# A corner table stored as two shifted halves, and later samples' moments through one buffer, in a four-layer image network

## The chip, the cores and the metric

The kernel runs on one core of a Trainium2 chip. The metric is the device time of one execution in microseconds; the input is four samples of 96 channels by 128 x 128 pixels in float32, all computed by that core in one launch.

The engines named below: PE (matrix multiplication and transposition; PEld is its weight load), DVE (vector), ACT (activations), POOL (here gathers and some elementwise work), and SP, which issues nearly all DMAs. Each engine runs its instructions in the order in which they were put into its queue.

## The reference, cut to what matters

Four residual layers, each on a group-normalised input. Layer 2 is a deformable 3 x 3 convolution, and the change lies in what feeds it.

```python
x = x + _L0_conv_ref(_gn(x), ...)   # convolution, gate, two scans over all pixels
x = x + _L1_conv_ref(_gn(x), ...)   # spatial and spectral branches, 3x3 convolution
x = x + _L2_conv_ref(_gn(x), ...)   # deformable 3x3 convolution
x = x + _L3_conv_ref(_gn(x), ...)   # mask, DCT, state-space scans, DCT back

def _L2_conv_ref(x, weight, bias, offset_w, offset_b, mask_w, mask_b):
    offset = _conv(x, offset_w, offset_b)
    mask = jax.nn.sigmoid(_conv(x, mask_w, mask_b))
    ...
    for k in range(K * K):
        i, j = (k // K, k % K)
        dy = offset[:, 2 * k]
        dx = offset[:, 2 * k + 1]
        py = base_y[None, :, None] + i * DIL + dy
        px = base_x[None, None, :] + j * DIL + dx
        samp = _bilinear(x, py, px) * mask[:, k][:, None]
        out = out + jnp.einsum('bchw,oc->bohw', samp, weight[:, :, i, j])
    return out + bias[None, :, None, None]
```

`_bilinear` weighs four neighbouring pixels: (y, x), (y, x+1), (y+1, x), (y+1, x+1), zero outside the image.

## The kernel before, in words

Per sample there is a front (layers 0 and 1 and the offsets of layer 2: `front`, line 652), a back (the gather of layer 2, the mask and the first DCT of layer 3: `back`, line 1410) and `layer3` (the scans). The main loop at the end of `tile_net_kernel` runs: the first front alone; then, for each sample b, its back together with the front of sample b+1 (and the last DCT of sample b-1), followed by its layer 3 alone. The last back has no front beside it.

Front and back are written as generators, and every operation is recorded by `Program.record`; a planner (`Program.issue`) then puts the operations of the two lanes into one order per engine, by its own costs and by each operation's planned place within its lane. The order is fixed when the program is built; on the chip each engine follows it. All recorded operations carry line 66 in the profile (DMAs line 426), so they are told apart by the tiles' names.

The steps that the change touches:

- `layer0`, lines 662 to 755. `moments` (679) loads an image in eight pieces of 96 x 2048 (tile `l0_xt`) and takes `bn_stats` of each 512 columns, four per piece. It runs first for sample 0, in its own pool of three buffers. Then, in the first front only, `next_moments` (743) does the same for samples 1 to 3 in the pool `l0a`, three buffers too, beside the convolution of layer 0 (`block`, 719), which loads its rows, and stores its two results `u_d` and `sz_d`, through the same SP queue.
- `offsets`, lines 1247 to 1408. It goes over eight blocks of 16 rows. Each block loads 18 rows (`rows`, two buffers), normalises them on DVE, and builds the corner table `quad_d` in DRAM: one entry of 4 x 96 channels (1536 B) for each of 127 x 128 pixels, in the order (y, x), (y, x+1), (y+1, x), (y+1, x+1). Through `q4` (1254) it is written with the pixel's column x on the partitions.
- For every pair of rows PE transposes each row twice, once from column 0 and once from column 1, into one PSUM tile `l2_pt` (two buffers). DVE copies both halves of a row into the first two quarters of the tile `l2_qt` (three buffers, 128 x 4 rows x 384), and ACT copies the same into the last two quarters of the row before. Each four rows are stored by one DMA, 32 a sample.
- Between these, PE computes the offset convolution (`l2_po`), transposes it (`l2_pu`), and DVE and ACT make from it the row of the table to read (`idx_d`) and the four weights of each tap (`w4_d`), in the order of the corners (lines 1396 to 1405).
- `gather`, lines 1421 to 1524. POOL reads, for each image row and tap, one table entry per pixel by an indirect DMA into `l2_g`; `weigh` (1448) multiplies the four corners by their weights on ACT and adds on DVE; the result is transposed and multiplied by the layer's weights. The indices, weights and residual of the next four rows are fetched on the SP queue (`l2_i`, `l2_v`, `l2_x`).

The store of four rows before, with its only view of the table:

```python
q4 = T.quad_d.rearrange("(y x) e -> x y e", x=W)
...
nc.sync.dma_start(
    out=q4[:, BR * i + r - 4 : BR * i + r, :], in_=last
)
```

Of the kernel before, what the change touches and what calls it, by code (L numbers as in the profile page):

```python
# [23 lines left out]
F32 = mybir.dt.float32  # L24
# [3 lines left out]
ALU = mybir.AluOpType  # L28
# [4 lines left out]
C, H, W = 96, 128, 128  # L33
# [61 lines left out]
def staggered(jobs, gap):  # L95


    jobs = iter(jobs)
    active, wait = [], 0
    while True:  # L100
        if wait <= 0:
            job = next(jobs, None)
            if job is not None:
                active.append(job)
                wait = gap
        wait -= 1
        if not active:
            return
        for job in list(active):
            if next(job, "end") == "end":  # L110
                active.remove(job)
                if not active:
                    wait = 0
            else:
                yield
# [405 lines left out]
BR = 16  # L521
# [4 lines left out]
class Net:  # L526
# [135 lines left out]
    def layer0(self, xin, T, beside, ahead):  # L662
        nc, a = self.nc, self.a
# [3 lines left out]
        with self.program.pool(name="l0w", bufs=1) as wp, self.program.pool(name="l0p", bufs=1, space=PSUM) as ps:  # L667
# [8 lines left out]
            wc = wp.tile([C, 9, C], F32, name="l0_wc")  # L676
            nc.sync.dma_start(out=wc, in_=a["l0_cwT"].unsqueeze(0).to_broadcast([C, 9, C]))

            def moments(pool, x, st):
                for i in range(8):  # L680
                    xt = pool.tile([C, 2048], F32, name="l0_xt", tag="xt")
                    nc.sync.dma_start(out=xt, in_=x[:, i * 2048 : (i + 1) * 2048])
                    yield
                    for t in range(4):
                        nc.vector.bn_stats(st[:, 4 * i + t, :], xt[:, t * CH : (t + 1) * CH])
                        yield

            if ahead is not None:
                with self.program.pool(name="l0s", bufs=3) as wa:
                    yield from moments(wa, xin, st0)  # L690
# [26 lines left out]
            with self.program.pool(name="l0a", bufs=3) as wa, self.program.pool("l3i", 2) as wt:  # L717

                def block(i):
                    xb, cols = self.rows(wa, xin, i, 3)  # L720
                    yield
                    yield
                    nc.vector.tensor_scalar(xb[:, cols], xb[:, cols], scale, shift, ALU.mult, ALU.add)
                    yield
                    for r in range(3):
                        pc = ps.tile([128, CH], F32, name="l0_pc", tag="a", bufs=2)
                        yield from self.conv9(pc, wc, xb, i, r)
                        u = wa.tile([128, CH], F32, name="l0_u", tag="u")
                        nc.scalar.activation(u, pc, AF.Silu, bias=cb[:, r : r + 1], scale=1.0)
                        self.spread_out(u_d, u, i, r)  # L730
                        pz = ps.tile([128, CH], F32, name="l0_pz", tag="b", bufs=1)
                        with self.program.abreast():
                            for p, g, c in self.shares(r):
                                nc.tensor.matmul(
                                    out=pz[p : p + 32], lhsT=winT[:, C + c : C + c + 32],
                                    rhs=xb[:, W + g * CH : W + (g + 1) * CH], start=True, stop=True,
                                )
                        yield
                        sz = wa.tile([128, CH], F32, name="l0_sz", tag="sz")
                        nc.scalar.activation(sz, pz, AF.Silu)  # L740
                        self.spread_out(sz_d, sz, i, r)

                def next_moments():
                    for x, mv in ahead:
                        st = wa.tile([C, NCH, 6], F32, name="l0_st", tag="st", bufs=2)
                        yield from moments(wa, x, st)
                        nc.vector.bn_aggr(mv, st.rearrange("c n s -> c (n s)"))
                        yield

                jobs = [staggered((block(i) for i in range(NB)), 12)]  # L750
                if beside:
                    jobs.append(beside(ps, wt))
                if ahead:
                    jobs.append(next_moments())
                yield from staggered(jobs, 1)
# [491 lines left out]
    def offsets(self, T):  # L1247


        nc, a = self.nc, self.a  # L1250
# [3 lines left out]
        q4 = T.quad_d.rearrange("(y x) e -> x y e", x=W)  # L1254
        NR = BR + 3
        with self.program.pool(name="l2w", bufs=1) as wp, self.program.pool(name="l2a", bufs=2) as wa, self.program.pool(
            name="l2p", bufs=1, space=PSUM
# [15 lines left out]
            def block(i):  # L1273
                xb, cols = self.rows(wa, T.x2, i, pad=PAD)
# [5 lines left out]

                n = min(BR, H - 1 - BR * i)
                qt = None
                for r in range(0, n + 1, 2):
                    if r % 4 == 0 and r < n:
                        last, qt = qt, wa.tile([128, 4, 4 * C], F32, name="l2_qt", tag="qt", bufs=3)
                    elif r % 4 == 0:
                        last = qt
                    else:
                        last = qt
                    k = min(2, n + 1 - r)  # L1290
                    pt = ps.tile([128, 2, 2 * C], F32, name="l2_pt", tag="b", bufs=2)
                    for j in range(k):
                        for x in range(2):
                            c0 = (1 + r + j) * W + x
                            nc.tensor.transpose(
                                pt[:, j, x * C : (x + 1) * C], xb[:, c0 : c0 + W], self.ident[:C, :C]
                            )
                    yield
                    up = min(k, n - r)
                    if up > 0:  # L1300
                        nc.vector.tensor_copy(qt[:, r % 4 : r % 4 + up, 0 : 2 * C], pt[:, :up])
                    if r % 4:
                        nc.scalar.copy(qt[:, 1 : 1 + k, 2 * C : 4 * C], pt[:, :k])
                    else:
                        if r:
                            nc.scalar.copy(last[:, 3, 2 * C : 4 * C], pt[:, 0])
                            nc.sync.dma_start(
                                out=q4[:, BR * i + r - 4 : BR * i + r, :], in_=last
                            )
                        if k > 1:  # L1310
                            nc.scalar.copy(qt[:, 0, 2 * C : 4 * C], pt[:, 1])
                if n % 4:
                    nc.sync.dma_start(
                        out=q4[:, BR * i + n - n % 4 : BR * i + n, :], in_=qt[:, : n % 4]
                    )

                ot = wa.tile([128, NR, 123], F32, name="l2_ot", tag="ot")
                if prev[0] is None:
# [7 lines left out]
                for g in range(4):  # L1326
                    po = ps.tile([123, 4, W], F32, name="l2_po", tag="a", bufs=2)
                    x3 = image(xb[:, :XB])
                    for m, x in enumerate((0, -1, 1)):
                        ca, cb = max(0, -x), min(W, W - x)  # L1330
                        nc.tensor.matmul(
                            out=po[:, :, ca:cb], lhsT=woff[:, x + 1].rearrange("c y k -> c (y k)"),
# [7 lines left out]
                    pt = ps.tile([128, 4, 123], F32, name="l2_pu", tag="b", bufs=2)  # L1340
# [5 lines left out]
                r0 = 1 if i == 0 else 0  # L1346
                nr = BR + (i == NB - 1) - r0
                K9 = nr * 9
# [10 lines left out]
                w4 = wa.tile([128, NR * 9, 4], F32, name="l2_w4", tag="w4")  # L1359
                first, wts = [], []  # L1360
# [35 lines left out]
                for m in range(2):  # L1396
                    wy = wts[0][m]
                    wy3 = wy.rearrange("w (r k) -> w r k", k=9)
                    nc.vector.tensor_tensor(wy3, wy3, mask[:, :nr], ALU.mult)
                    for j in range(2):  # L1400
                        nc.vector.tensor_tensor(w4[:, :K9, 2 * m + j], wy, wts[1][j], ALU.mult)
                nc.sync.dma_start(
                    out=T.w4_d[:, row0 * 36 : row0 * 36 + 4 * K9],
                    in_=w4[:, :K9].rearrange("p k q -> p (k q)"),
                )
                yield

            yield from staggered((block(i) for i in range(NB)), 28)

    def back(self, T, alone=False):  # L1410
# [1040 lines left out]
```

## Time and profile before

| What | Value |
|---|---|
| Time, median of three runs | 14923.91 us (14919.98 to 14983.37) |
| The profiled execution's own time | 14956.1 us |
| Its span | 14954.0 us |
| Mean granted clock of PE | 0.894 |
| PE / DVE / ACT / POOL busy | 82% / 76% / 59% / 69% |
| Packets of the hardware queue (SP) | 1,013,872, 1972.56 MB, 45.8% of 16 DMA engines |
| Packets of the software queue (POOL's gathers) | 298,368, 906.38 MB, 20.5% |
| Stores of the corner table | 32 a sample; 768 KB for four rows |
| Offsets stage of sample 0 | first store issued at 1123.8, last at 1297.0 us; gather from 1318.0 us |
| Stores of samples 1, 2, 3 | 2916.0 to 3273.2, 6455.9 to 6850.0, 9974.9 to 10333.4 us |
| Gathers of samples 1, 2, 3 start | 4817.0, 8344.9, 11826.4 us |
| `bn_stats` of `l0_xt` for samples 1 to 3 | 51.8 to 153.9 us |

How to read the profile: "busy" is the time in which an engine worked on an instruction; waiting is not in it. In a group of instructions the columns are engine, operation, output <- inputs, shapes and count, then the busy time in us and the mean of one in ns, then the idle time of the engine just before these instructions and what ended it. Tile names stand without their digits: `l_qt` is `l2_qt`, `l_xt` is `l0_xt`; `l_pt<-ident,rows` are the transpositions for the corner table and `l_pt<-ident,l_sm` those of the gather. Names of the same letters in two layers fall together. A DMA's time on SP is that of its issue alone.

### The profile page before, as it was taken

Reading aid. Unit: us, or ns where it says so; the run is one execution under the profiler, and the core shown is the slowest. Engines: PE = TensorE matmul, PEld = TensorE weight load, DVE = VectorE, ACT = ScalarE, POOL = GpSimd, SP = SyncE. Lnnn points to the kernel's source line nnn. Section 1 sums busy time; section 2 is a strip of 40 time slices with the busy share of each in tenths; the row PEclk is TensorE's granted clock in tenths of the full one; section 3 lists DMA queues with packets and bytes.
Section 4 is the critical chain, followed back from the end, with each engine's and each line's share of the span. In section 5 each row is a group of like instructions: output and inputs, shape, how many; then the busy total and the mean of one; then the engine's idle time right before and its main releaser. Section 6 shows DMA issues by size and latency. Waiting matters only on the chain. (4 is left out here: it accounts for less than half of the span.)

```text
span 14954.0 us, 175601 instructions
## 1 busy us (share of the span) xinstructions
PE 12275.2 (82%) x48112; PEld 5769.1 (39%) x48112; DVE 11311.0 (76%) x21823; ACT 8881.9 (59%) x21508; POOL 10357.0 (69%) x7904
## 2 busy tenths in 40 slices
PE   7897787879998978878999878887999744459998
PEld 3353344343333434443333334534333422233334
DVE  4625686678998587677999678667999765558997
ACT  3614675556665586555666467555666465546664
POOL 2103747748998755765999774774999877758997
PEclk9998898979999988978999989888999855569999
DMA  6445658766666758875666766876666755556676
GB/s 163 135 131 187 185 168 249 233 205 177 188 196 192 243 169 225 236 221 162 194 189 193 222 202 176 255 237 186 192 189 196 213 171 168 166 153 184 187 199 193
DMA packets 1313229, 2890.16 MB, mean 193 GB/s; under 512 B 281008, under 2 KB 767600, under 8 KB 1197936
## 3 DMA queue, kind: packets, MB, share of 16 engines
q1 hardware_dynamic: 1013872, 1972.56, 45.8%
q0 software_dynamic: 298368, 906.38, 20.5%
q8 instruction: 381, 6.24, 0.2%
q14 instruction: 608, 4.98, 0.1%
HBM read 2455.55 MB, written 422.58 MB: 192 GB/s over the span
## 5 line engine op out<-in xcount | busy, mean ns | idle before, releaser
L66 POOL DMA_INDIRECT l_g<-quad_d,l_i x4608 | 4664.4, 1012 | 2516.9 <-issue 1330.6
L66 POOL TENSOR_TENSOR l_hc<-l_h,l_cl 128x1024 f32<-128x1024 f32 x1536 | 3608.5, 2361 | 288.6 <-DVE l_h L66 264.1
L66 PE MATMUL l_py<-l_hc,ident 128*128 128x512 f32 x6144 | 3073.9, 611 | 181.2 <-POOL l_hc L66 177.9
L66 DVE TENSOR_TENSOR_SCAN l_h<-l_dA,l_carry,l_dB 128x512 f32<-128x512 f32 x2304 | 2861.4, 1265 | 1.7
L66 ACT ACTIVATE l_dA<-l_dl,l_al 128x512 f32<-128x512 f32 x2304 | 1637.4, 718 | 1111.6 <-DVE l_h L66 1102.6
L66 DVE SCALAR_TENSOR_TENSOR l_sm<-l_g,l_v,l_sm 128x96 f32<-128x96 f32 x4608 | 1480.5, 322 | 1039.4 <-ACT l_sm L66 1004.6
L66 ACT ACTIVATE l_sm<-l_g,l_v 128x96 f32<-128x96 f32 x4608 | 1680.1, 369 | 646.8 <-DMA l_g<-quad_d,l_i 612.3
L66 ACT ACTIVATE l_part<-l_g,l_v 128x96 f32<-128x96 f32 x4608 | 1656.6, 364 | 213.3 <-DVE l_sm L66 213.1
L66 PEld LDWEIGHTS l_py<-l_hc,ident 128*128 128x128 f32 x6144 | 1135.2, 192 | 1348.3 <-issue 828.0
L66 PE MATMUL l_pc<-l_sT,l_wk 128*96 128x256 f32 (+1 forms) x3584 | 1238.3, 470 | 449.9 <-ACT l_sT L66 447.4
L66 DVE TENSOR_TENSOR l_dB<-l_du,l_pB 128x512 f32<-128x512 f32 x2304 | 1492.2, 677 | 48.7 <-POOL l_du L66 27.7
L66 PE MATMUL l_pB<-l_bc,pick 128*128 128x512 f32 x2304 | 1402.1, 637 | 136.1 <-DVE l_dB L66 122.1
L66 DVE SCALAR_TENSOR_TENSOR l_part<-l_g,l_v,l_part 128x96 f32<-128x96 f32 x4608 | 1477.8, 321 | 43.8 <-ACT l_part L66 43.1
L66 PE MATMUL l_pt<-ident,l_sm 128*128 128x128 f32 (+1 forms) x3584 | 793.7, 326 | 750.7 <-DVE l_sm L66 746.2
L66 POOL TENSOR_TENSOR l_dP<-l_du,l_cl 128x512 f32<-128x512 f32 x768 | 978.1, 1274 | 100.9 <-DMA l_cl<-bc_d 71.6
L66 DVE TENSOR_TENSOR_SCAN l_h<-l_dQ,l_carry,l_dP 128x512 f32<-128x512 f32 x768 | 971.1, 1264 | 58.1 <-POOL l_dP L66 54.7
L66 PEld LDWEIGHTS l_pc<-l_sT,l_wk 128*96 128x96 f32 (+1 forms) x3584 | 643.2, 199 | 962.4 <-ACT l_sT L66 552.2
L66 PEld LDWEIGHTS l_pt<-ident,l_sm 128*128 128x128 f32 (+1 forms) x3584 | 521.7, 164 | 1140.1 <-DVE l_sm L66 874.7
L66 ACT COPY l_sT<-l_pt 128x512 f32<-128x512 f32 (+1 forms) x1024 | 522.3, 522 | 626.8 <-PE l_pt L66 625.5
L66 POOL TENSOR_TENSOR l_du<-l_du,l_dl 96x512 f32<-96x512 f32 x256 | 339.9, 1328 | 792.8 <-DVE l_dl L66 482.5
L66 PE MATMUL l_pc<-rows,l_wc 96*32 96x508 f32 (+3 forms) x6912 | 841.7, 612 | 46.7 <-DVE rows L66 46.7
L66 PEld LDWEIGHTS l_pB<-l_bc,pick 128*128 128x128 f32 x2304 | 438.5, 191 | 1062.2 <-DVE l_dB L66 834.5
(274 smaller groups left out, 19887.2 us busy)
## 6 DMA issues: line engine op xcount, KB each, us to landing
l_cl<-bc_d SPq DMA_DIRECT2D x512, 1280.0 KB
l_cl<-bc_d SPq DMA_DIRECT2D x512, 640.0 KB
quad_d<-l_qt SPq DMA_DIRECT2D x124, 768.0 KB
l_g<-quad_d,l_i POOLq DMA_INDIRECT x4608
x<-l_x SPq DMA_DIRECT2D x352, 192.0 KB
l_uc<-u_d SPq DMA_DIRECT2D x256, 192.0 KB
l_x<-x SPq DMA_DIRECT2D x224, 192.0 KB
l_xs<-x SPq DMA_DIRECT2D x116, 256.0 KB
```

The lines of the kernel that those rows point to most:

```text
L66: ins = op(*args, **kw).ins
```

## The change

There are three edits.

1. `moments` takes the number of buffers, and `next_moments` calls it with one instead of three.
2. In `offsets` each row is transposed once, four rows into one PSUM tile (128 x 4 x 96, as many bytes as before). The tile `l2_qt` holds four rows of 192 channels, (y, x) and (y+1, x), half its former size, still in three buffers. DVE copies the rows, ACT the rows one further down. The table's entry has the order (y, x), (y+1, x), (y, x+1), (y+1, x+1). Each four rows are stored by the new function `put` with three DMAs on the SP queue: the tile from partition 0 into the first half of the entries, the tile from partition 1 (127 partitions) into the second half of the entries of columns 0 to 126, and the last partition into the second half of column 127, whose entries no index names, since the index is held to columns 0 to 126.
3. The weights are written in the new order of corners.

```diff
-            def moments(pool, x, st):
+            def moments(pool, x, st, bufs=3):
                 for i in range(8):
-                    xt = pool.tile([C, 2048], F32, name="l0_xt", tag="xt")
+                    xt = pool.tile([C, 2048], F32, name="l0_xt", tag="xt", bufs=bufs)
                     nc.sync.dma_start(out=xt, in_=x[:, i * 2048 : (i + 1) * 2048])
...
-                        yield from moments(wa, x, st)
+                        yield from moments(wa, x, st, 1)
...
-                for r in range(0, n + 1, 2):
-                    if r % 4 == 0 and r < n:
-                        last, qt = qt, wa.tile([128, 4, 4 * C], F32, name="l2_qt", tag="qt", bufs=3)
-                    elif r % 4 == 0:
-                        last = qt
-                    else:
-                        last = qt
-                    k = min(2, n + 1 - r)
-                    pt = ps.tile([128, 2, 2 * C], F32, name="l2_pt", tag="b", bufs=2)
+
+                def put(tile, r0, k):
+                    rows = slice(BR * i + r0, BR * i + r0 + k)
+                    nc.sync.dma_start(out=q4[:, rows, 0 : 2 * C], in_=tile[:, :k])
+                    nc.sync.dma_start(out=q4[0 : W - 1, rows, 2 * C : 4 * C], in_=tile[1:W, :k])
+                    nc.sync.dma_start(out=q4[W - 1 : W, rows, 2 * C : 4 * C], in_=tile[W - 1 : W, :k])
+
+                for r in range(0, n + 1, 4):
+                    k, up = min(4, n + 1 - r), min(4, n - r)
+                    last = qt
+                    pt = ps.tile([128, 4, C], F32, name="l2_pt", tag="b", bufs=2)
                     for j in range(k):
-                        for x in range(2):
-                            c0 = (1 + r + j) * W + x
-                            nc.tensor.transpose(
-                                pt[:, j, x * C : (x + 1) * C], xb[:, c0 : c0 + W], self.ident[:C, :C]
-                            )
-                    yield
-                    up = min(k, n - r)
+                        c0 = (1 + r + j) * W
+                        nc.tensor.transpose(pt[:, j, :], xb[:, c0 : c0 + W], self.ident[:C, :C])
+                    yield
                     if up > 0:
-                        nc.vector.tensor_copy(qt[:, r % 4 : r % 4 + up, 0 : 2 * C], pt[:, :up])
-                    if r % 4:
-                        nc.scalar.copy(qt[:, 1 : 1 + k, 2 * C : 4 * C], pt[:, :k])
-                    else:
-                        if r:
-                            nc.scalar.copy(last[:, 3, 2 * C : 4 * C], pt[:, 0])
-                            nc.sync.dma_start(
-                                out=q4[:, BR * i + r - 4 : BR * i + r, :], in_=last
-                            )
-                        if k > 1:
-                            nc.scalar.copy(qt[:, 0, 2 * C : 4 * C], pt[:, 1])
+                        qt = wa.tile([128, 4, 2 * C], F32, name="l2_qt", tag="qt", bufs=3)
+                        nc.vector.tensor_copy(qt[:, :up, 0:C], pt[:, :up])
+                    if r:
+                        nc.scalar.copy(last[:, 3, C : 2 * C], pt[:, 0])
+                        put(last, r - 4, 4)
+                    if k > 1:
+                        nc.scalar.copy(qt[:, : k - 1, C : 2 * C], pt[:, 1:k])
                 if n % 4:
-                    nc.sync.dma_start(
-                        out=q4[:, BR * i + n - n % 4 : BR * i + n, :], in_=qt[:, : n % 4]
-                    )
+                    put(qt, n - n % 4, n % 4)
...
-                        nc.vector.tensor_tensor(w4[:, :K9, 2 * m + j], wy, wts[1][j], ALU.mult)
+                        nc.vector.tensor_tensor(w4[:, :K9, 2 * j + m], wy, wts[1][j], ALU.mult)
```

## The prediction

> **What bounds the kernel now.** I first cut the span into stages (busy time of each engine by stretch: after the span, PE, PEld, DVE, ACT and POOL with counts, then granted clock, DMA share, GB/s).
>
> ```profile
> span 14954.0 us, 175601 instructions
> ...
> 1100.00:1320.00 220.00, 166.47 (x641) 95.77 (x633) 140.37 (x371) 81.56 (x207) 1.70 (x2) 0.75 0.51 168
> 1320.00:2880.00 1560.00, 1303.15 (x6882) 592.15 (x6882) 1062.29 (x2793) 968.97 (x2788) 1041.23 (x993) 0.91 0.71 206
> 2880.00:3300.00 420.00, 302.42 (x1122) 162.02 (x1122) 312.26 (x967) 257.17 (x778) 228.53 (x224) 0.76 0.69 217
> ...
> 3400.00:4800.00 1400.00, 1297.00 (x3188) 529.74 (x3188) 1340.39 (x1486) 924.36 (x1732) 1287.54 (x704) 0.98 0.66 190
> ```
>
> No engine bounds the whole. The reader is to see the first row: sample 0's offsets stage, alone on the core, no engine full, DMA at half its share. For samples 1 to 3 the same stage is mixed into the end of the previous sample's gather (2880 to 3300 and two like it); there POOL's gathers set much of the pace. The layer-3 scans (3400 to 4800) contain nothing that the change touches. So I read the offsets stage: the tile that changes, its PE work in the first front, and the DMA queue.
>
> ```profile
> L66 ACT COPY l_qt<-l_pt x380: 294/318/498, 1119.3 to 10332.2; 128x192 f32<-128x192 f32 x121, 128x384 f32<-128x384 f32 x69
> L66 DVE COPY l_qt<-l_pt x256: 339/550/579, 1118.7 to 10331.8; 128x384 f32<-128x384 f32 x128
> L426 SPq DMA_DIRECT2D quad_d<-l_qt x128: 359/370/1164, 1123.8 to 10333.4; - x128
> ...
>   DMA quad_d<-l_qt: 1.7, 2
> ```
>
> ```profile
> L66 PE MATMUL l_pt<-ident,rows 96*128 96x96 f32 x270 | 41.5, 298 | 24.6 <-ACT l_qt L66 17.6 <-DVE rows L66 6.9
> ```
>
> ```profile
> SPq L426 <- DVE l_idx L66: 75.9, 7, 11.2
> SPq L426 <- ACT l_qt L66: 54.4, 32, 3.8
> ```
>
> ```profile
> 1123.79 14.21 SPq L426 DMA_DIRECT2D quad_d<-l_qt  x4
> 1143.91 0.32 SPq L426 DMA_DIRECT2D rows<-x  x1
> 1153.81 0.34 SPq L426 DMA_DIRECT2D idx_d<-l_idx  x1
> 1156.04 0.33 SPq L426 DMA_DIRECT2D w_d<-l_w  x1
> 1156.94 5.20 SPq L426 DMA_DIRECT2D quad_d<-l_qt  x3
> ```
>
> What matters is the 1.7 us: in the whole run the three buffers of `qt` made engines wait 1.7 us for a store. The stores are free today; SP waits for the copies (54.4 us), not the copies for SP. A store's 512 packets of 1536 B are shared evenly: the trace's completion marks show sixteen reports for the store issued at 1123.79, 3.35 to 3.55 us later, and its packets take 65 ns (median; mean 69). 32 packets on each engine are 2.1 us; the other 1.3 us is latency.
>
> **The change, part by part.**
>
> *Transpositions and copies (saved).* 270 transpositions become 135: of 41.5 us PE in the first front 20.8 go, and perhaps half of the 24.6 us that they wait. DVE has 32 copies where it had 64 (0.55 us each: -17.6 us a sample). On ACT 192 columns take 0.32 us and 384 take 0.48, so 96 plus 288 take some 0.64 per four rows, 20 us a sample for 33 now. All three engines have room in this stage (166, 140 and 82 of 220 us), so this is worth at most the transpositions, 33 us in the first front, and less where the gather runs.
>
> *The stores (added).* Each `put` issues three DMAs for one. SP: 64 more per sample at 0.37 us, 24 us of a queue that spends far more waiting: nothing. The first (128 partitions) and the third (one partition, four rows) are harmless. The second, `tile[1:W]` into `q4[0 : W - 1]`, has 127 partitions, and the trace shows what an odd number of partitions does. Counting engine reports of one load each: 128 or 96 partitions report sixteen times; 65 (`k_fd`) thirteen; 12 (`rest`) twelve; 8 (`l1_m2`) eight; 6 partitions of 2 pieces (`l0_xpd`) six; 41 (`l2_boff`) **once**. The count is the largest divisor of the outer dimension up to 16. That the one engine works serially shows too: the 41 descriptors reported 1.76 us after issue, a single one (`l1_b2`) after 1.22, so 40 more cost 0.55 us, 14 ns each. 127 is prime like 41: one engine moves all 127 x 4 = 508 packets of 768 B.
>
> The Trainium skill (DMA: Bandwidth & Descriptors, "Why a DMA increments its semaphore by 16 and not by 1") states this rule and names 127 partitions as a case with one engine; it speaks against the change. The same page, under "Specifications", has about 27 GiB/s per engine: by that figure a put would take 13.5 us and the forecast would be some 16,000 us (four times 208 us less), but the 1536 B rows here reach only 23.6 GB/s.
>
> *Price of a 768 B packet.* No store of this size is in the trace. Idx stores of 576 B took 29 ns, the quad stores 65 at 1536 B; on the line between, 768 B are 36.2. In proportion to 1536 B it would be 32.5 (lower bound); the 768 B loads of weights had a mean of 51 (upper bound). I take 36.2 times the 69.4/65 of mean to median above: 38.6 ns, nearest because it is the same direction and tile. So the second put takes 508 x 38.6 = 19.6 us on its engine, where a store is issued every 5.4 us now (1123.8 to 1297.0, 32 of them). Per sample: 127 x 127 packets = 623 us, plus that engine's 1/16 of the first put, 1016 packets, 39 us, plus 1 us of the third: **663 us**.
>
> *Where it is paid.* With three buffers the fourth `qt` copy on DVE waits for the landing of the first store. Behind it in DVE's order stand the offset arithmetic and, from sample 1 on, the weighing (`l_sm`, `l_part`) of the previous sample's gather; behind these POOL's `l_g`, whose buffers the weighing frees. On SP the rows, index, weight and `l_v` DMAs queue up behind up to three puts, because they too have a part on that engine. So the stage runs at the pace of one engine, which must also do its share of everything else.
> First front: DMA share 0.51 over 201 us (1117 to 1318) is 102 us, less 70 of today's stores (16,256 packets x 69 ns / 16) leaves 32. 663 + 32 = 695 us after 1123.8, so the last store lands at 1819, not at 1300: +518; up to 18 us of that was idle before the gather's start at 1318: **+510**, taken in the middle.
> Samples 1 to 3: windows 2890 to 3292, 6435 to 6870 and 9950 to 10350 have 402, 435 and 400 us at DMA shares 0.69, 0.65 and 0.72: 277, 283 and 288 us, less 70 each. 663 + 207 - 402 = **+468**; 663 + 213 - 435 = **+441**; 663 + 218 - 400 = **+481**.
> In this the saved PE, DVE and ACT time is worth nothing: the one DMA engine covers it.
>
> *Moments through one buffer.* The loads `l_xt` of the later samples now alternate with their four `bn_stats` (2.47 us a group). A load lands some 6.4 to 7.2 us after issue where little else ran, with a handover a cycle of 9.3 to 10 us; 24 from 43.4 end between 266 and 284, where they end at 154 now. The convolution beside them keeps PE until 267, and that is their cover; without it the whole 130 us would count. Behind the waiting load on SP stand the `u_d`, `sz_d` stores and `rows` loads, all with three buffers (8 us per piece of work, 24 us of room): no cost. 0 to 25 us; I take 10, as most of the span between 266 and 284 is past the end at 267.
>
> *Order of corners and weights.* Four products of 0.42 us to the same stride, gathered rows still 1536 B: nothing.
>
> *Sum.* 510 + 468 + 441 + 481 + 10 = +1910 on the profiled 14,954, which lies 0.2% over the median 14,923.9. From the median: **16,830 us**, 12.8% more. With 32.5 ns each sample has 558 for 663: -420 in all, and 0 for the moments: 16,400. With 51 ns it has 877: +856, and 25 for the moments: 17,700.
>
> **Rivals.**
> *A, not slower: the shifted put is spread.* If it reached four engines or more, a put took 4.9 us or less, under the 5.4 us between stores, and hid again. Then -33 us in the first front, some -5 us (a quarter of the transpositions, in the stretch after the gather) for each later sample, +10 for the moments: 14,924 - 38 = 14,886 us, 0.25% less. For it: 16 engines have 8 us more of packets, easily hidden. Against: the single report of the 41-partition load. 5%; a coin toss shared between no change and, if the waits go entirely, faster.
> *B: only the first front pays.* If DVE's order let the gather run past the waiting copies, three stages would hide it beside 1,500 us of gather: 14,924 + 520 = 15,444. Against: the order of each engine is fixed, and three buffers hold 12 of 127 rows. 5%.
> *C: the gather starves as well.* `l_i` is fetched about 22 us before use (issued at 3046.2, half a group of 36 gathers ahead); behind three puts it lands 59 us later. Should the 37 us not overlap with the engine's backlog, once in each of eight blocks and three samples, 890 us come on top: 17,720. Against: the puts still queued keep that engine working meanwhile. 12%.
>
> **The numbers.** The forecast has 78%, A 5, B 5, C 12. A measurement here tells about 0.5%, 75 us, from no change. Slower by more 0.94, within 0.04, faster 0.02. The range goes from 16,200, below the lower bound since a part of the other DMAs may fall outside the stage, to 17,800, above the upper bound and C; outside it lie A, B and the ends of the others.
>
> **What would show it.** Right: `quad_d<-l_qt` three times as often; waits for DMA `quad_d` by DVE's `l_qt` of some 500 us in the first front and not 1.7 us; the gather of sample 0 starting near 1,820; one report, some 20 us or more after issue, for the shifted put; a DMA share in the stage far lower than now; the layer-3 stages as long as before. Wrong: sixteen reports for the shifted put (A), packets of 768 B much off 38.6 ns (size), POOL idle for `l_i` in the store stage (C), a later stage that keeps its 400 us (B).

## The result, and the profile after

The changed kernel takes 16,508.9 us (median of 6 runs, 16,500.4 to 16,513.8), the kernel before 14,943.7 us in the same series (6 runs): 1.104 times as long, 95% interval 1.1025 to 1.1058. The forecast was 16,830 us in a range of 16,200 to 17,800.

The head of the page of after, and its hardware queue (packets, MB, share of 16 engines):

```profile
span 16505.9 us, 174690 instructions
...
PE 12289.5 (74%) x47572; PEld 5748.6 (35%) x47572; DVE 11243.4 (68%) x21695; ACT 8821.9 (53%) x21374; POOL 10339.9 (63%) x7904
...
q1 hardware_dynamic: 1079532, 1972.56, 41.6%
```

The bytes are the same, the packets 6.5% more, and the DMA engines are on the average less busy than before. So more data is not the cause. The same four stages as before, each stretched or moved to where it lies now (span, busy time of PE, PEld, DVE, ACT, POOL, granted clock, DMA share, GB/s):

```profile
1100.00:1730.00 630.00, 150.72 (x522) 81.13 (x513) 126.01 (x339) 67.91 (x175) 2.15 (x3) 0.59 0.19 59
1730.00:3250.00 1520.00, 1295.42 (x6820) 592.15 (x6821) 1054.06 (x2765) 965.79 (x2763) 1023.60 (x979) 0.91 0.72 210
3250.00:4060.00 810.00, 293.97 (x1088) 167.91 (x1088) 307.94 (x967) 244.91 (x769) 240.44 (x241) 0.64 0.38 116
4160.00:5570.00 1410.00, 1298.70 (x3190) 529.23 (x3189) 1344.03 (x1503) 922.51 (x1729) 1286.09 (x703) 0.98 0.66 189
```

The first row shows sample 0's store stage: the work of the engines has shrunk a little (PE 166 to 151 us, DVE 140 to 126), the stretch has grown from 220 to 630 us, and the DMA share has fallen from 0.51 to 0.19. The third row, sample 1's stores beside the end of sample 0's gather, shows the same (420 to 810 us, 0.69 to 0.38). Gather and layer 3, rows two and four, have nearly the same work and rates as before (the second row's stretch was cut 40 us shorter than before's).

Who waits there for whom, in sample 1's stores (between 3290 and 4060 us; each line gives the us in total, the times and the longest):

```profile
DVE l_qt L66 <- DMA quad_d<-l_qt: 351.9, 21, 23.6
POOL l_g L66 <- DVE l_part L66: 289.7, 13, 48.0
```

Before, between 2890 and 3290 us, the second of these lines was

```profile
POOL l_g L66 <- DVE l_part L66: 15.7, 8, 13.6
```

So DVE stands before the copies for the table, and POOL's gathers then wait for the weighing that stands behind them on DVE.

The tile that changed, and what it waits for in the whole run:

```profile
L426 SPq DMA_DIRECT2D quad_d<-l_qt x384: 234/528/26657, 1121.5 to 11808.6; - x192
L66 ACT COPY l_qt<-l_pt x252: 214/376/419, 1120.9 to 11773.5; 128x96 f32<-128x96 f32 x63, 128x288 f32<-128x288 f32 x63
L66 DVE COPY l_qt<-l_pt x128: 457/558/562, 1120.3 to 11771.9; 128x384 f32<-128x384 f32 x124, 128x288 f32<-128x288 f32 x4
...
  DMA quad_d<-l_qt: 2360.3, 143
```

Three times as many stores, and 2360 us of waiting for them, where it was 1.7. In the first front alone (waits between 1110 and 1730 us, and the transpositions' group between 1105 and 1730 us):

```profile
DVE l_qt L66 <- DMA quad_d<-l_qt: 362.1, 26, 18.2
ACT l_qt L66 <- DMA quad_d<-l_qt: 283.6, 21, 20.6
```

```profile
L66 PE MATMUL l_pt<-ident,rows 96*128 96x96 f32 x135 | 24.7, 317 | 270.5 <-ACT l_qt L66 263.6 <-DVE rows L66 6.9
```

The transpositions are halved (135 for 270, 24.7 us of work for 41.5), and PE now stands 270 us before them where it stood 24.6. Why a wait is 18 us long is to be seen on SP, whose timeline (start, length, instructions merged) reads:

```profile
1121.48 69.82 SPq L426 DMA_DIRECT2D quad_d<-l_qt  x12
1191.40 0.39 SPq L426 DMA_DIRECT2D rows<-x  x1
1191.89 0.36 SPq L426 DMA_DIRECT2D idx_d<-l_idx  x1
1192.34 0.38 SPq L426 DMA_DIRECT2D w_d<-l_w  x1
```

Twelve stores, four puts, occupy SP for 69.8 us, where four stores took 14.2; `rows`, indices and weights stand behind. A report is, as in the prediction, a completion mark of the trace, one for each DMA engine that had a part of the transfer. The completion marks of the first and second put in the trace (us after issue):

```
issued at 1121.48  128 partitions   16 reports, 2.42 to 2.69
issued at 1121.90  127 partitions   a mark at 0.52, then one report at 20.03
issued at 1122.31    1 partition    its own issue takes 15.48 us
issued at 1137.90  128 partitions   16 reports, 2.4 to 5.1
issued at 1138.33  127 partitions   a mark at 0.69, then one report at 21.43
issued at 1138.91    1 partition    its own issue takes 16.71 us
issued at 1155.72  128 partitions   the next put: a period of 17.8 us
```

The 127-partition store has a first mark at its issue, sooner than the load of one descriptor landed before (1.22 us), and then one report where the store of 128 has sixteen: one engine has all of the data. Between 1126 and 1136 us its packets of 768 B start every 33.0 ns (median; the tenth and ninetieth percentile are the same), and the trace gives each 36 ns, so that they overlap. 508 x 33.0 ns are 16.8 us; with 32 packets, a sixteenth of the first store, they are 17.8 us, the period that is seen. In the first front the last report of the 127-partition store comes 21.5 us after issue in the median (17.0 to 24.9).

Where the time went, in us (the gather's start for sample 0; then, for samples 0 to 2, from the first gather to layer 3's first `l_cl<-bc_d`, a stretch that holds the next sample's stores):

| | before | after | more | forecast |
|---|---|---|---|---|
| gather of sample 0 starts | 1318.0 | 1727.2 | 409 | 510 |
| gather 0, with the stores of sample 1 | 2088.9 | 2432.2 | 343 | 468 |
| gather 1, with those of sample 2 | 2114.5 | 2491.8 | 377 | 441 |
| gather 2, with those of sample 3 | 2071.6 | 2487.4 | 416 | 481 |
| gather 3, no stores | 1651.8 | 1655.0 | 3 | 0 |
| first load of the scans of layer 0 (moments) | 271.0 | 268.9 | -2 | 10 |

The first four rows hold 1545 of the 1552 us by which the two profiled spans differ.

### The profile page after: what moved, and what is told of

Its sections match the earlier page's. It is cut to its first block, busy times and chain, and to the rows that moved or that the text cites. A ratio compares the mean times of both kernels' runs of the same rounds, so it can differ in the third digit from the quotient of the medians.

```text
span 16505.9 us, 174690 instructions
## 1 busy us (share of the span) xinstructions
PE 12289.5 (74%) x47572; PEld 5748.6 (35%) x47572; DVE 11243.4 (68%) x21695; ACT 8821.9 (53%) x21374; POOL 10339.9 (63%) x7904
## 5 line engine op out<-in xcount | busy, mean ns | idle before, releaser
L66 DVE COPY l_qt<-l_pt 128x384 f32<-128x384 f32 (+1 forms) x128 | 70.7, 553 | 1382.7 <-DMA quad_d<-l_qt 1355.9
L66 ACT COPY l_qt<-l_pt 128x288 f32<-128x288 f32 (+1 forms) x252 | 76.1, 318 | 1590.6 <-DMA quad_d<-l_qt 1004.4
```

Of the source, the lines that this page charges most:

```text
L66: ins = op(*args, **kw).ins
```

## Experiments

The theory: 127 has no divisor up to 16 but one, so one engine moves the shifted put, at one packet every 33 ns. In the edits, `tile` and `q4` are as in the diff of the change. The kernels with 112 and 15 and with 122 and 5 partitions, the first with 128, and the moments alone ran on a chip where the kernel before took 14,944 us; the others ran on two chips where it took 16,572 and 16,729 us. There the gather stages are longer: the last gather, which has no stores beside it, lasts 1,892 to 1,945 us in these runs and 1,647 to 1,655 in the others. So of these runs the ratio to the kernel before beside them, or the difference from it, and the start of sample 0's gather are read.

**The shifted put over more engines.** In place of one DMA from 127 partitions, two, from 112 and 15:

```diff
-nc.sync.dma_start(out=q4[0 : W - 1, rows, 2 * C : 4 * C], in_=tile[1:W, :k])
+nc.sync.dma_start(out=q4[0:112, rows, 2 * C : 4 * C], in_=tile[1:113, :k])
+nc.sync.dma_start(out=q4[112 : W - 1, rows, 2 * C : 4 * C], in_=tile[113:W, :k])
```

> The changed kernel, its shifted put cut into 112 and 15 partitions (sixteen and fifteen engines). Theory (one engine moves the 127-partition put at 33 ns a packet, nothing else costs): a put takes some 2.3 us, under the 5.4 us between stores of before; the store stages go back to 200 us for sample 0 and 400 to 435 us for the others; waits for quad_d by l_qt under 20 us; 14,870 us, 14,840 to 14,950. Rival (the halved packets, 768 B for 1536, or the three and more DMAs on the SP queue are what costs): still over 15,500 us.

Measured: 14,846.0 us, ratio to the kernel before 0.993 (in brackets, here and below, its 95% interval: [0.9917, 0.9943]); the gather of sample 0 starts at 1299.5 us. The lines of its tile in the whole run:

```profile
L426 SPq DMA_DIRECT2D quad_d<-l_qt x512: 310/600/2942, 1123.0 to 10178.6; - x171
...
  DMA quad_d<-l_qt: 95.4, 41
```

It issues still more stores (512), the longest issue on SP is 2.9 us where it was 26.7, and the 112 and the 15 partitions of the first put report sixteen and fifteen times, within 3.7 us of their issue. The waits of `l_qt` for `quad_d` are 95.4 us and not under 20, so this part of the expectation was missed; in the first front they are 6.1 us on DVE and 7.6 on ACT, where they were 362 and 284. The whole loss is gone: neither the number of DMAs nor the halved packets cost it, only the number of engines.

**One DMA from 128 partitions.** Partition 0 belongs one entry earlier, to column 127 of the row above, which no index names. So the whole tile can be stored one entry earlier; only row 0 needs its partition 0 left out, and the last row its column 127 filled:

```diff
+q4s = T.quad_d[W - 1 : (H - 1) * W - 1, :].rearrange("(y x) e -> x y e", x=W)
...
-nc.sync.dma_start(out=q4[0 : W - 1, rows, 2 * C : 4 * C], in_=tile[1:W, :k])
+nc.sync.dma_start(out=q4s[:, y + j - 1 : y + k - 1, 2 * C : 4 * C], in_=tile[:, j:k])
```

Here y is the first row of the put, and j is 1 for the put with row 0 and else 0; row 0 is stored from 112 and 15 partitions.

> The changed kernel, its shifted put as one DMA of 128 partitions, written one table entry earlier, so that partition 0 falls into an entry that no index names (row 0 alone in 112 and 15 partitions). Theory: sixteen engines as in the cut put, two DMAs a store, 14,860 us, 14,830 to 14,950, so up to 0.5% under the kernel before, from half the transpositions and copies. Rival (saved PE, DVE and ACT work is worth nothing in these stages): 14,924 us, no change.

Measured: 14,840.0 us, ratio 0.9927 [0.9913, 0.994]; 67 stores a sample, gather at 1290.7 us. This is the lowest median on this chip, 0.7% under the kernel before, though its interval and that of the first experiment overlap. The rival, that the saved work is worth nothing, falls here: the saved work of the change is thus worth some 100 us once the stores run on all engines. On another chip:

> The same kernel as in the first look (shifted put as one DMA from all 128 partitions, written one entry earlier), here beside the other three for comparison. It was at 0.9927 [0.9913, 0.994] of the kernel before; the theory expects 0.992 to 0.994, about 14,840 us, and sample 0's gather start near 1,291 us.

It measured 0.9951 [0.9931, 0.9971], with the gather at 1286.2 us. The ratio lies above the expected 0.992 to 0.994, but the intervals of the two chips overlap; the first front is as expected.

**Two engines.** 122 and 5 partitions, cut as in the first experiment, use 2 and 5 engines:

> The changed kernel, its shifted put cut into 122 and 5 partitions, two engines and five. Theory: the busiest engine has 61 x 4 = 244 packets of 33 ns, 8.1 us, 1.1 us of the first put and 0.1 of the small one: 9.3 us a store, 294 us a sample. Sample 0: 294 + 32 us, gather from about 1,452 us (1318 before, 1727 after). Others: 294 + 207, 213, 218 less 402, 435, 400 us = +99, +72, +112. In all 15,340 us, 15,200 to 15,450. Rival (any put of few engines blocks the SP queue for a fixed 17 us): about 16,500 us.

Measured: 15,467.2 us in one run, gather of sample 0 at 1456.3 us. The 122 partitions of the first put report twice, 11.3 and 11.4 us after issue; the five report five times. SP's timeline:

```profile
1121.73 36.11 SPq L426 DMA_DIRECT2D quad_d<-l_qt  x16
1157.93 0.39 SPq L426 DMA_DIRECT2D rows<-x  x1
```

Four puts hold SP for 36.1 us, about half of 69.8. The first front is as expected; the later samples lose 85, 121 and 152 us to the kernel before, together 75 us more than expected, so the whole is just above its range. The rival, a fixed 17 us for any put of few engines, is refuted.

**The moments alone.** The kernel before with only the first edit:

```diff
-yield from moments(wa, x, st)
+yield from moments(wa, x, st, 1)
```

> The kernel before with the moments of samples 1 to 3 through one buffer, nothing else. Prediction on record: +10 us (0 to 25). After the trace of the changed kernel, where the last bn_stats ended at 241 us and the scans began at 269 (271 before): 0 us, between -5 and +5; no change. Rival (the moments' loads hold up the SP queue): 15 us or more, scans starting after 285 us.

Measured: ratio 1.0002 [0.9988, 1.0016]. Its waits between 40 and 270 us:

```profile
ACT l_u L66 <- PE l_pc L66: 153.7, 21, 11.8
DVE l_st L66 <- DMA l_xt<-in_x: 126.0, 24, 7.2
```

The 24 loads are awaited 126 us in all, and the last `bn_stats` comes at 246.9 us instead of 153.9; but the first load of the scans is issued at 267.7 (271.0 before), and before that ACT waits for the convolution's PE as well. The cover holds; the rival's start after 285 us did not come.

**Four engines.** 124 and 3 partitions (4 and 3 engines), twice:

> The changed kernel, its shifted put cut into 124 and 3 partitions, four engines and three. Theory: the busiest engine has 31 x 4 = 124 packets of 33 ns, 4.1 us, with its parts of the other puts 5.3 us a store, 168 us a sample, just under the 173 us that the stores of sample 0 took before. Gather of sample 0 from about 1,327 us (1299 with the put cut in 112 and 15, 1456 with two engines); the other stages up to 30 us longer than with 112 and 15: 14,900 us, 14,860 to 14,970. Rival (few engines hurt however many): 15,100 us or more.

> Shifted put cut into 124 and 3 partitions, 4 engines and 3 engines. Theory (one engine moves a 768 B packet every 33 ns; 124 x 4 packets on 4 engines are 4.1 us, under the 5.4 us between stores): hidden but for some of it, sample 0's gather start between 1,310 and 1,350 us (the first look had 1,347), and the whole between 14,850 and 14,960 us. Rival (any store on fewer than 16 engines is paid in full): sample 0's store stage 4.1 us times 32 longer than with 112 and 15 partitions, gather start at 1,400 us or later, and the whole near 15,250 us.

Measured: ratios 1.0063 [1.0046, 1.008] and 1.0069 [1.0047, 1.0091]; the gather of sample 0 at 1347.2 and 1347.6 us. The store stage of sample 0 in the second:

```profile
1100.00:1350.00 250.00, 137.54 (x497) 75.70 (x489) 124.20 (x339) 67.90 (x175) 2.06 (x2) 0.73 0.50 148
```

The start at 1347 is 20 us over the first expectation and at the top of the second's range, which was set with the first start known. The whole misses both: it is 0.6% to 0.7% dearer than the kernel before and, beside the kernel with 128 partitions on the same chip, 1.2% dearer. Four engines are not enough, but what the rivals named, 15,100 us in the first and a start at 1,400 us in the second, isn't reached either.

**The kernel before with 127 partitions.** No edit of the change, only each store of 1536 B entries cut in 127 and 1:

```diff
-nc.sync.dma_start(out=q4[:, BR * i + r - 4 : BR * i + r, :], in_=last)
+nc.sync.dma_start(out=q4[0 : W - 1, rows, :], in_=last[0 : W - 1])
+nc.sync.dma_start(out=q4[W - 1 : W, rows, :], in_=last[W - 1 : W])
```

> The kernel before, with each store of the corner table cut into 127 partitions and 1, nothing else. Theory (the partition count alone makes one engine do the store, and a packet costs by its bytes): 508 packets of 1536 B at some 60 ns are 30 us a store and 968 us a sample; gather of sample 0 from about 2,130 us, the other three stages +770, +750, +790 us: 18,050 us, 17,700 to 18,400. By packets alone (33 ns each): 16,400 us. Rival (the halves, the row of three DMAs or the shift by a partition cause the loss): 14,930 us.

Measured: 19,601.6 us in one run, 3,029 more than the kernel before beside it (18,050 stood for 3,126 more than 14,924); gather of sample 0 at 2144.8 us. In its stage, with the same work as before:

```profile
1100.00:2140.00 1040.00, 182.50 (x671) 101.84 (x663) 141.23 (x366) 83.28 (x206) 0.00 (x0) 0.56 0.10 35
```

DMA share 0.10, 35 GB/s. Packets of 1536 B start every 61.0 ns there (median between 1140 and 1500 us). So the partition count does it alone, and the price goes nearly with the bytes: 33.0 and 61.0 ns.

**Six buffers.** The changed kernel, twice:

```diff
-qt = wa.tile([128, 4, 2 * C], F32, name="l2_qt", tag="qt", bufs=3)
+qt = wa.tile([128, 4, 2 * C], F32, name="l2_qt", tag="qt", bufs=6)
```

> The changed kernel with six buffers of qt for three. Theory (one DMA engine sets the pace): sample 0's gather starts within 15 us of 1727, since all its stores must land; the other samples can leave up to three more stores, 54 us, to drain after their stage: 16,430 us, 16,340 to 16,520. Rival (the three buffers set the pace, and with more the store hides): sample 0's gather before 1,600 us, 16,000 us or less.

> The changed kernel with six buffers for the store tile in place of three. Theory (one DMA engine sets the pace, the buffers only pass it on): sample 0's gather start at 1,727 us plus or minus 15 and the whole between 16,400 and 16,560 us. Rival (the short ring of buffers is the stall): the first front gets back 100 us or more and the whole falls below 16,200 us.

Measured: the gather of sample 0 starts at 1730.4 and 1733.7 us, within 7 us of the 1727.2 with three buffers; the stores of the later samples last 691 to 697 us in both, where they lasted 686 to 701. The whole, 17,974 and 18,138 us (8% over the kernel before beside them), can't be held against the totals that were expected, since the changed kernel with three buffers was not run on those chips. The waits of the second run between 1110 and 1730 us show where the stall went:

```profile
ACT l_qt L66 <- DVE l_qt L66: 365.2, 17, 58.9
...
DVE rows L66 <- DMA rows<-x: 338.3, 7, 58.1
```

DVE's wait for a free `l_qt` is 16.6 us there and no longer 362; it waits nearly as long for the next `rows`, whose load stands on SP behind twelve stores. More buffers move the wait by a step in the chain and don't shorten it.

**The shifted put from POOL's software queue.**

```diff
-nc.sync.dma_start(out=q4[0 : W - 1, rows, 2 * C : 4 * C], in_=tile[1:W, :k])
+nc.gpsimd.dma_start(out=q4[0 : W - 1, rows, 2 * C : 4 * C], in_=tile[1:W, :k])
```

> The changed kernel, its shifted put of 127 partitions issued by POOL on the software queue, nothing else. If that queue spreads the 127 partitions over all engines: sample 0's gather from 1,290 to 1,320 us; beside the gathers each of 32 puts takes 1 to 2 us of POOL and waits for its copies in POOL's order: 14,950 us, 14,850 to 15,150. If it too puts all on one engine: sample 0's gather after 1,650 us and 16,300 us or more.

Measured: 18,441.6 us in one run, 1,869 more than the kernel before beside it; gather of sample 0 at 1671.5 us. Its row in the tile's view:

```profile
L66 POOL DMA_DIRECT2D quad_d<-l_qt x128: 4341/4608/5597, 1122.2 to 13548.0; - x128
```

Neither expectation fits: the second's figures came true (a start after 1,650 us), but not for its reason. The first such put does report sixteen times, fifteen of them 12.4 to 14.2 us after issue and one at 31.2; in the first front the last report of these puts comes 29 to 37 us after issue. Each costs POOL 4.6 us, in the later samples ahead of gathers: their stores last 940 to 976 us. Why the last report is so late stays open, and how much of the loss is due to it and how much to POOL's time was not separated.

**What the gain of 100 us comes from.** The kernel with 128 partitions, but each row transposed twice into the same place, so that PE has its old work again:

```diff
-nc.tensor.transpose(pt[:, j, :], xb[:, c0 : c0 + W], self.ident[:C, :C])
+for _ in range(2):
+    nc.tensor.transpose(pt[:, j, :], xb[:, c0 : c0 + W], self.ident[:C, :C])
```

> As the kernel with the shifted put from 128 partitions, but each row is transposed twice into the same place, so that TensorE does the 254 transpositions a sample of the kernel before, while VectorE and ScalarE keep the fewer copies. Theory 1: the gain of some 100 us comes from TensorE's 127 transpositions less: then the first front gives most of its gain back (sample 0's gather start from 1,291 to 1,305 to 1,318 us) and the whole is near 14,900 to 14,940 us. Theory 2: it comes from the copies of VectorE, which stand in one order with the weighing of the previous sample's gather: then the whole stays within 25 us of the kernel with single transpositions, near 14,840 to 14,865 us, with at most 15 us later in sample 0.

Measured: ratio 0.9945 [0.9927, 0.9963] beside 0.9951 [0.9931, 0.9971] with single transpositions; gather of sample 0 at 1287.4 us beside 1286.2. The first front with single and with double transpositions:

```profile
1100.00:1290.00 190.00, 138.94 (x533) 76.51 (x525) 124.04 (x341) 67.85 (x175) 3.00 (x3) 0.80 0.64 198
```

```profile
1100.00:1290.00 190.00, 144.08 (x664) 82.00 (x656) 123.94 (x340) 67.34 (x175) 2.05 (x2) 0.87 0.64 196
```

131 more matmuls are 5 us more of PE's time, at a granted clock of 0.87 for 0.80, and the stage is as long. So the gain is not TensorE's, and the moments alone gave none above. What is left is the fewer, larger copies of DVE and ACT and their handovers (DVE 32 for 64 a sample), the stores in two halves, and the order that the planner makes of them. The copies are the likeliest, but that they make the gain was not shown alone.

## Why the prediction was right, and what was off

**The mechanism was right.** One engine serves the shifted put: one report of data, 20.0 and 21.4 us after issue in the first two puts; waits of `l_qt` for `quad_d` 362 us on DVE in the first front (some 500 were named, for a stretch that is 100 us shorter than forecast); DMA share 0.19. The experiments with 112 and 15, and with 128 partitions, take the loss away; the kernel before gets one of 3,029 us by 127 partitions alone. Rival B is refuted by the three later stretches, which pay 343 to 416 us each. Rival C, a gather starved of `l_i`, would have come on top of the engine's own time; the later stretches, at the measured price of a packet, hold 34 us more in all than the engine's own time, not 890. In sample 1's stores POOL waits 289.7 us for DVE's weighing, as was forecast, and for no load of `l_i`. The Trainium skill (DMA: Bandwidth & Descriptors, "Why a DMA increments its semaphore by 16 and not by 1") has the rule; the marks agree for 127 partitions (one report), 122 (two), 112 (sixteen) and 15 (fifteen). It also says that the issuing sequencer adds the engines left out at once; the mark at the issue fits that, but the trace shows a mark without its size.

**The term that was mis-sized is the price of a packet**, 38.6 ns. The line between 576 and 1536 B gave 36.2, and the trace has 36 as the time of one; but it was then raised by the ratio of mean to median, and a packet's time was taken for the engine's pace. Packets start every 33.0 ns, before the last is done. 5.6 ns x 17,145 packets are 96 us a sample. With 33.0 ns the forecast's own steps give +413 in the first front and +372, +345 and +385 later, 1515 in all; measured were 409, 343, 377 and 416, 1545 in all. The lower bound in proportion to 1536 B, 32.5 ns, came so near by luck: it is half of 65 ns, the time recorded for one packet and not a spacing. Packets of 1536 B start every 61.0 ns, and half of that is 30.5. For the same reason the 23.6 GB/s that the prediction read for rows of 1536 B is too low: by their spacing one engine moves 25.2 GB/s, and 23.3 with rows of 768 B.

**SP's part was put at nothing**, since only the time of 64 more issues was counted. SP was held 16.7 us by each put instead (see the end). That `rows`, indices and weights queue up behind the puts was named, and in the first front the hold adds nothing that can be told apart: the engine's own time gives 413 us, and 409 were lost.

**The moments** cost nothing, not 10 us: the cover that was named, PE's convolution until 267 us, reaches past the last `bn_stats` at 241.5. The loads were issued every 8.3 us on the average, not every 9.3 to 10.

**Saved work worth nothing under the DMA:** right for this kernel. But rival A's saving without that cover, 38 us net of the 10 for the moments, was too small: the kernels with all engines gain some 100. In the first front it was near (33 forecast, 19 and 27 measured), though not by the transpositions that it priced; for the later samples it had 5 us each, and the kernel with 128 partitions gained 48, 52 and 8 in the gathers that hold their stores.

**Rival A's threshold was wrong too.** "Four engines or more" was to hide the put, since 4.9 us lie under the 5.4 us between stores. That engine also has its part of the first put, 32 packets or 1.06 us, and 32 us of other transfers a front, 1.0 us a put. With 508, 248 and 128 shifted packets of 33 ns at most on the busiest engine (of the second DMA's packets 4 are counted in), the sum for 32 puts is 602 us for one engine, 328 for two and 201 for four; between the first and the last issue of sample 0 there passed 581, 321 and 213 us. With 112 and 15 partitions, at most 28 and 4 packets an engine, the sum is 100, and the 158 us that passed are no longer the DMA's.

## What to carry to other kernels

Before cutting a partition off a DMA, look at the count that is left: a prime such as 127 gave one engine the whole transfer, while 112 and 15, or a shift that keeps all 128, used fifteen or sixteen engines and landed in the first front after 3.3 to 4.5 us (medians) instead of 21.5. The completion marks tell it from one run: a single late report where sixteen are usual means one engine, and a stage whose DMA share falls while engines wait for DMA is its sign. Twice the buffers did not help here: the engine had as many packets to move, and the issuing queue was held as well. Price an engine by the spacing of its packets and with everything else that it has to move.

## What the runs showed that was not expected

SP itself is held. In the first front the DMA that follows a one-engine put takes 16.7 us to issue in the median (12.4 to 20.2), 7.7 us behind a two-engine put (5.1 to 11.3) and 4.4 behind one of four engines (2.7 to 6.7), where the median issue of a store in the kernel before was 0.37 us. These medians are near the time of one put's shifted packets on its engine: 508, 244 and 124 x 33.0 ns are 16.8, 8.1 and 4.1 us. So everything on SP's queue waits, not only the tile's buffers. Why SP is held stays open.

The same kernel (the shifted put from 128 partitions) took 14,840 us on one chip and 16,639 on another. The stage of its first gather, on the first chip and then on the second (columns as in the stages above):

```profile
1290.00:2850.00 1560.00, 1301.11 (x6887) 594.83 (x6887) 1066.27 (x2804) 972.60 (x2789) 1050.44 (x1008) 0.91 0.73 209
```

```profile
1286.00:3240.00 1954.00, 1533.41 (x6894) 658.09 (x6895) 1070.60 (x2810) 975.33 (x2792) 1054.45 (x1008) 0.85 0.59 167
```

With the same instructions, DVE, ACT and POOL are as long busy, PE is busy 18% longer at a lower granted clock, and the stage is 25% longer; the first front (gather at 1290.7 and 1286.2) and layer 3 of sample 0 (from its first `l_cl<-bc_d` to the next gather, 1420 and 1411 us) are not. The waits of the whole run on the second chip have a line that those on the first do not have at all:

```profile
ACT l_sT L66 <- remote: 1113.2, 149, 34.9
```

"remote" means that the trace of this core names nothing that ended the wait. The packets of the gathers are not slower there: their median is 175 ns in both stretches. What holds the engines there stays open.
